# A four-layer graph network on one core: aggregations as seven products with the adjacency as left factor, three graphs in flight in tiles handed out by the plan

## The chip, the core and the metric

The kernel runs on one core of a Trainium2 chip. The engines are TensorE (PE; its weight loads are shown as PEld), VectorE (DVE), ScalarE (ACT), GpSimd (POOL) and SyncE (SP, which issues the large DMAs). The metric is the device time of one execution in microseconds (us). Everything is float32.

## The reference

32 graphs of 512 nodes with 256 features each go through four layers; each layer multiplies by the graph's own 512 x 512 adjacency matrix. `_layernorm` has no gain or shift.

```
x = _layernorm(x + mlp0((1 + eps) * x + adj @ x))           # relu(h @ W1 + b1) @ W2 + b2, 256-512-256
x = _layernorm(x + prelu(adj @ (x @ W.T + b)))              # 256-256
h = layer_norm(x, gamma, beta)
x = _layernorm(x + (x + relu((adj @ h) @ W_rel + b_rel + h @ W_root)))
x = _layernorm(x + silu(rmsnorm((epsilon * x + adj @ x) @ W1 + b1) * w) @ W2 + b2)   # 256-1024-256
```

## The kernel before

The kernel writes no instruction directly. It describes operations (`plan.do`, `plan.move`), and `Plan.add` derives what depends on what from the tiles that an operation reads and writes. This is done by grains: 128 columns of a tile, PSUM tiles included. Matmuls into one bank are in addition kept in order (`ordered=o.bank`). `Plan.order` then lays all operations out in time with a duration for each kind (`matmul_time`, `vector_time` and so on), always giving an engine the operation of the oldest graph that is ready; an operation that two engines can do goes to the one that would finish first. The operations are issued in the order found, so each engine's queue has a fixed order, and the semaphores follow from that order. In the profile all operations therefore bear one line, L180, and are told apart by their tiles.

Two graphs are in flight. Each has its own `Set` of named tiles (adjT, x, aT, h, t, part0 and others); graph b uses set b % 2. `load_graph` issues x and four chunks of the adjacency on SP. PSUM has eight tiles `ps`, one bank of 128 x 512 each, and the plan gives an operation the bank that comes free first.

A layer begins with an aggregation. `aggregate` is called twice, for each half of the features. It sums four matmuls, 128 x 128 of x as stationary operand and 128 x 512 of the transposed adjacency as moving operand, into one bank, and a copy takes the bank to the tile aT (features on partitions, 512 nodes). Layers 0 and 3 need the adjacency with something added on its diagonal: GpSimd copies the four 128 x 128 diagonal blocks to dg, adds, restores and adds again. Layer 1 also sums the adjacency's rows on GpSimd. After the aggregation come dense matmuls with the layer's weights, element work on VectorE and ScalarE, and a norm (`Norm`: statistics, a power on GpSimd, and four `tensor_scalar` on VectorE in `scaled`).

Layer 3 already does its two dense products by the seven-product scheme of Strassen and Winograd. `seven` calls `product` for m1 to m7, `take` where a partial sum has to be kept in SBUF, and `put` where a block of the result is made; weights are combined once (`weight_sums`), the right factor for each graph. Its three accumulators x, y and z are three banks; m1, m6, m7 and m4 are added up in x one after the other. In the first product of layer 3 an accumulator is a whole bank (two blocks of 256 columns), in the second half of a bank is used.

Of the kernel before, what the change touches and what calls it, by code (L numbers as in the profile page):

```python
# [16 lines left out]
GRAIN = 128  # L17
BANKS = 8


def span(ap):

    n = 1
    for d in ap.shape[1:]:
        n *= d
    return n

# [42 lines left out]
@dataclass  # L70
class Op:


    rank: tuple
    ways: dict
    banks: list
    behind: int = 0
    ready: dict = field(default_factory=dict)
    then: list = field(default_factory=list)
    start: float = 0.0  # L80
    way: str = ""


class Bank:


    def __init__(self):
        self.index = None
        self.left = 0
        self.until = 0.0  # L90


class Part:


    def __init__(self, bank, model, path):
        self.bank, self.model, self.path = bank, model, path
        self.shape = model.shape

    def __getitem__(self, i):  # L100
        return Part(self.bank, self.model[i], (*self.path, i))

    def place(self, tiles):
        shape, *path = self.path
        v = tiles[self.bank.index]
        if shape:
            v = v.rearrange("p (i n) -> p i n", i=shape)
        for i in path:
            v = v[i]
        return v  # L110


class Plan:
# [3 lines left out]
    def __init__(self, nc, banks):  # L117
        self.nc = nc
        self.tiles = banks
        self.ops = []  # L120
        self.place = 0
        self.writer, self.readers = {}, {}

    def bank(self, split=0):
        model = self.tiles[0]
        if split:
            model = model.rearrange("p (i n) -> p i n", i=split)
        return Part(Bank(), model, (split,))

    def grains(self, x):  # L130
        key = x.bank if isinstance(x, Part) else x.tensor.name
        ap = x.model if isinstance(x, Part) else x
        starts = [ap.offset]
        dims = list(ap.ap)[1:]
        for step, n in dims[:-1]:
            starts = [s + step * i for s in starts for i in range(n)] if step else starts
        step, n = dims[-1]
        return {
            (key, g)
            for s in starts  # L140
            for g in range(s // GRAIN, (s + step * (n - 1)) // GRAIN + 1)
        }

    def add(self, ways, out, ins, ordered=None):
        op = Op((self.place, len(self.ops)), ways, [])
        self.ops.append(op)
        before, behind_end = set(), set()
# [4 lines left out]
        for g in reads:  # L152
            if g in self.writer:
                behind_end.add(self.writer[g])
        for g in reads - writes:
            self.readers.setdefault(g, []).append(len(self.ops) - 1)
        for g in writes:
# [3 lines left out]
            self.writer[g] = len(self.ops) - 1  # L161
        me = len(self.ops) - 1
        before = (before | behind_end) - {me}
        for i in before:
            self.ops[i].then.append((me, i in behind_end))
        op.behind = len(before)
        for x in (out, *ins):
            if isinstance(x, Part) and x.bank not in op.banks:
                op.banks.append(x.bank)
                x.bank.left += 1  # L170

    def do(self, ways, out, *args, ordered=None, **kw):

        ins = [x for x in (*args, *kw.values()) if isinstance(x, (bass.AP, Part))]

        def issue(engine, method, more):
            def put(x):
                return x.place(self.tiles) if isinstance(x, Part) else x

            getattr(getattr(self.nc, engine), method)(  # L180
                put(out), *(put(x) for x in args), **{k: put(x) for k, x in kw.items()}, **more
# [4 lines left out]
                e: (times, lambda e=e, method=method, more=more: issue(e, method, more))  # L186
                for e, (method, times, more) in ways.items()
# [4 lines left out]
    def move(self, engine, out, src, times, tile_in=None):  # L192

        self.add(
            {engine: (times, lambda: getattr(self.nc, engine).dma_start(out, src))},
            None if tile_in is not None else out,
            [] if tile_in is None else [tile_in],
        )

    def order(self):  # L200
        free = dict.fromkeys(("tensor", "vector", "scalar", "gpsimd", "sync"), 0.0)
        occupant = [None] * BANKS
        open_ops = {i for i, op in enumerate(self.ops) if not op.behind}
        done = []
        while open_ops:
            best = {}
            spare = min(
                (0.0 if o is None else o.until if not o.left else 1e12, k)
                for k, o in enumerate(occupant)
            )  # L210
            for i in open_ops:
                op = self.ops[i]
                wait = spare[0] if any(b.index is None for b in op.banks) else 0.0
                at = {e: max(free[e], wait, op.ready.get(e, 0.0)) for e in op.ways}
                way = min(at, key=lambda e: at[e] + sum(op.ways[e][0]))
                best.setdefault(way, []).append((at[way], op.rank, i))
            t, engine = min((min(c)[0], e) for e, c in best.items())
            assert t < 1e11, "no bank comes free"
# [5 lines left out]
            for b in op.banks:  # L224
                if b.index is None:
                    b.index = spare[1]
                    occupant[b.index] = b
                b.left -= 1
                b.until = max(b.until, t + busy + then)
            for n, reads in op.then:  # L230
                o = self.ops[n]
                o.behind -= 1
                for e in o.ways:
                    if e != engine:
                        at = t + busy + then + HAND[e]
                    elif e == "tensor" or not reads:
                        at = 0.0
                    else:
                        at = t + busy + then + HAND[e]
# [10 lines left out]
def tile_gnn_stack(ctx: ExitStack, tc: tile.TileContext, a: dict, out: bass.AP):  # L250
# [36 lines left out]
    STREAMS = 2  # L287
# [4 lines left out]
    plan = Plan(nc, [psum.tile([P, N], F32, tag=f"ps{i}", name=f"ps{i}") for i in range(BANKS)])  # L292


    def on_vector(method, n, **more):
        return {"vector": (method, vector_time(n), more)}

    def either(method, n, **more):
        return {
            "vector": (method, vector_time(n), more), "gpsimd": (method, gpsimd_time(n), more)  # L300
        }

    def mm(o, lhsT, rhs, first, last):
        n = rhs.shape[-1]
        ways = {"tensor": ("matmul", matmul_time(n), dict(start=first, stop=last, skip_group_check=True))}
        plan.do(ways, o, lhsT, rhs, ordered=o.bank)

    def flip(o, x):
        ways = {"tensor": ("transpose", flip_time(P), {})}
        plan.do(ways, o, x, ident, ordered=o.bank)  # L310

    def act(o, x, func, **kw):
        plan.do({"scalar": ("activation", scalar_time(span(o)), dict(func=func))}, o, x, **kw)

    def copy(o, x):
        plan.do(
            {
                "scalar": ("activation", scalar_time(span(o)), dict(func=AF.Copy)),
                "vector": ("tensor_copy", vector_time(span(o)), {}),
            },  # L320
            o, x,
        )

    def add(o, x, y, ways=on_vector):
        plan.do(ways("tensor_add", span(o)), o, x, y)

    def sub(o, x, y, ways=on_vector):
        plan.do(ways("tensor_sub", span(o)), o, x, y)

    def mul(o, x, y):  # L330
        plan.do(on_vector("tensor_mul", span(o)), o, x, y)

    def ts(o, x, s1, s2, op0, op1=None):
        more = dict(op0=op0) if op1 is None else dict(op0=op0, op1=op1)
        plan.do(on_vector("tensor_scalar", span(o), **more), o, x, s1, s2)

    def stt(o, x, s, y, op0, op1):
        plan.do(on_vector("scalar_tensor_tensor", span(o), op0=op0, op1=op1), o, x, s, y)

    def on_gpsimd(method, n, **more):  # L340
        return {"gpsimd": (method, gpsimd_time(n), more)}

    def inv_sqrt(o, x):
        n = span(o)
        plan.do(
            {"gpsimd": ("tensor_tensor", power_time(n), dict(op=ALU.pow))}, o, x, mhalf[:, 0:n]
        )

# [18 lines left out]
    def weight(name):  # L367
        w = a[name]
        t = constant(name, [P, w.shape[0] // P, w.shape[1]])
        plan.move("sync", t, w.rearrange("(c p) f -> p c f", p=P), move_time(w.shape[0] * w.shape[1] / 256))  # L370
# [11 lines left out]
    class Set:  # L382
# [3 lines left out]
        def __init__(self, number):  # L386
            self.number = number
            self.slots = {}

        def __call__(self, slot, shape):  # L390
            size = 1
            for n in shape:
                size *= n
            if slot not in self.slots:
                self.slots[slot] = work.tile(
                    [P, SLOTS[slot]], F32, tag=f"{slot}_{self.number}", name=f"{slot}{self.number}"
                )
            t = self.slots[slot][:, 0:size]
            if len(shape) == 2:
                t = t.rearrange("p (i n) -> p i n", i=shape[0])  # L400
            return t

        def tok(self, slot):
            return self(slot, [NC, D])

        def feat(self, slot, n=DC):
            return self(slot, [n, N])

    SLOTS = dict(
        adjT=NC * N, x=NC * D, dg=N, xb=NC * D, aT=DC * N, r=NC * D, h=FC3 * N, x2=NC * D,  # L410
# [406 lines left out]
```

## Time and profile before

| What | us |
|---|---|
| median of 3 runs (2618.21 to 2622.77) | 2622.53 |
| the profiled execution | 2623.28 |
| its span, first to last instruction | 2621.4 |
| aggregation matmuls, "ps<-adjT,x", 2048 records, busy | 941.6 |
| mean length of one such record | 0.598 |
| all of DVE, busy | 1779.3 |
| all of POOL, busy | 790.8 |
| all of ACT, busy | 696.4 |

An f32 matmul leaves two records, each with a weight load of its own. Records of matmuls overlap: each lasts from its start until its last column has left the array, while the next one begins earlier. What a matmul costs is therefore read from one start to the next. The granted TensorE clock is 0.994 of full speed on average.

### The profile page before, as it was taken

The numbers are of one execution on the slowest core, as the hardware profiler recorded it, in microseconds if no ns is written. First come the engines' busy times: TensorE is split into PE (matmuls) and PEld (weight loads), VectorE is DVE, ScalarE is ACT, GpSimd is POOL, SyncE is SP. The second block draws the span as 40 slices with busy tenths as digits, with TensorE's granted clock in tenths as the row PEclk, the third lists the DMA queues.
The fourth block names the chain that finished last, engine by engine and source line by source line (L and its number), as shares of the span: only waits on it lengthen the run. The fifth ranks groups of instructions, "written<-read, shape, count | busy, mean of one in ns | idle before, by whom it ended". The sixth has DMA issues, their size and how long they took to land.

```text
span 2621.4 us, 30535 instructions
## 1 busy us (share of the span) xinstructions
PE 2578.0 (98%) x11400; PEld 1807.3 (69%) x11400; DVE 1779.3 (68%) x3956; ACT 696.4 (27%) x1186; POOL 790.8 (30%) x1063
## 2 busy tenths in 40 slices
PE   7999999999999999999999999999999999999996
PEld 4766667666777677676767776666766677767765
DVE  4666667766676666766667666666776667666675
ACT  1231232322223222232213322123232222322222
POOL 3233232333332233322332313323233333223311
PEclk9999999999999999999999999999999999999998
DMA  3000000000001000000100100100010000010000
GB/s 117 25 33 33 9 32 25 33 33 33 9 25 33 33 33 9 33 33 25 33 12 29 33 25 33 33 9 33 25 33 33 33 9 25 33 33 33 9 9 9
DMA packets 34884, 73.54 MB, mean 28 GB/s; under 512 B 6832, under 2 KB 9648, under 8 KB 34736
## 3 DMA queue, kind: packets, MB, share of 16 engines
q1 hardware_dynamic: 30576, 71.05, 8.1%
q8 instruction: 90, 1.47, 0.2%
q10 hardware_dynamic: 4160, 0.54, 0.1%
q14 instruction: 58, 0.48, 0.1%
HBM read 54.80 MB, written 16.78 MB: 27 GB/s over the span
## 4 chain that ended last, share of the span: by engine, by line
PE 91%; DVE 6%; ACT 1%; POOL 1%; issue 1%; DMA 0%; POOLq 0%; ACTq 0%; DVEq 0%
PE ps L180 91%; DVE t L180 2%; POOL rstd L180 1%; ACT part L180 1%; DVE r L180 1%; DVE st L180 1%; DVE mv L180 0%; DVE h L180 0%; DVE x L180 0%; DMA L_gnn_b_c<-in_L_gnn_b_dram 0%; DVE ve L180 0%; ACT h L180 0%; DMA adjT<-in_adj_dram 0%; DVE part L180 0%; ACT u L180 0%
## 5 line engine op out<-in xcount | busy, mean ns | idle before, releaser
L180 PE MATMUL ps<-adjT,x 128*128 128x512 f32 x2048 | 941.6, 598 | 21.5 <-POOL adjT L180 13.6
L180 PEld LDWEIGHTS ps<-adjT,x 128*128 128x128 f32 x2048 | 376.2, 192 | 389.0 <-issue 323.9
L180 POOL TENSOR_TENSOR rstd<-ve,mhalf 128x4 f32<-128x4 f32 (+1 forms) x160 | 191.5, 1197 | 918.4 <-DVE ve L180 916.3
L180 PEld LDWEIGHTS ps<-L_gnn_W,h 128*128 128x128 f32 x2560 | 391.2, 192 | 107.3 <-issue 57.8
L180 PE MATMUL ps<-L_gnn_W,h 128*128 128x128 f32 (+1 forms) x2560 | 441.5, 318 | 4.1 <-ACT h L180 2.8
L180 PE MATMUL ps<-aT,L_gnn_W 128*128 128x512 f32 (+1 forms) x1024 | 361.1, 486 | 0.0
L180 DVE COPY aT<-ps 128x512 f32<-128x512 f32 x194 | 133.8, 690 | 256.7 <-PE ps L180 256.7
L180 ACT ACTIVATE part<-ps,L_gnn_b_c 128x256 f32<-128x256 f32 x384 | 157.2, 471 | 547.8 <-PE ps L180 547.8
L180 DVE TENSOR_SCALAR x<-r,mv,rstd 128x256 f32<-128x256 f32 x512 | 249.0, 541 | 72.1 <-POOL rstd L180 72.1
L180 PEld LDWEIGHTS ps<-aT,L_gnn_W 128*128 128x128 f32 x1024 | 193.5, 190 | 135.8 <-issue 123.4
L180 POOL TENSOR_TENSOR xb<-x,L_gnn_b 128x256 f32<-128x256 f32 x256 | 186.5, 751 | 205.8 <-DVE part L180 106.0
L180 DVE TENSOR_TENSOR h<-ps,part 128x512 f32<-128x512 f32 x192 | 132.8, 691 | 134.3 <-PE ps L180 74.4
L180 ACT ACTIVATE h<-ps,L_gnn_b_c 128x256 f32<-128x256 f32 (+1 forms) x256 | 141.8, 579 | 289.1 <-PE ps L180 259.8
L180 ACT ACTIVATE h<-h,L_gnn_rms_weight_c 128x512 f32<-128x512 f32 x256 | 168.8, 714 | 155.6 <-DVE h L180 154.8
L180 DVE BATCH_NORM_STATS2 st<-r 128x6 f32<-128x256 f32 x512 | 206.9, 409 | 3.9
L180 DVE TENSOR_TENSOR h<-h,ps 128x512 f32<-128x512 f32 x256 | 161.3, 683 | 2.3 <-PE ps L180 2.3
L180 POOL TENSOR_TENSOR adjT<-dg,loop 128x128 f32<-128x128 f32 x256 | 120.8, 472 | 139.6 <-PE ps L180 129.9
L180 POOL COPY adjT<-dg 128x128 f32<-128x128 f32 x128 | 76.9, 603 | 213.7 <-PE ps L180 213.7
L180 PE MATMUL ps<-t,L_gnn_W 128*128 128x256 f32 x512 | 140.0, 386 | 0.8 <-DVE h L180 0.8
L180 DVE TENSOR_TENSOR t<-ps,u 128x512 f32<-128x512 f32 x64 | 44.3, 692 | 141.1 <-PE ps L180 141.1
L180 PE MATMUL ps<-t,A 128*128 128x256 f32 x512 | 134.7, 386 | 2.1
L180 PE MATMUL ps<-L_gnn_W_root,h 128*128 128x256 f32 x512 | 121.1, 379 | 0.2 <-ACT h L180 0.2
(79 smaller groups left out, 3011.5 us busy)
## 6 DMA issues: line engine op xcount, KB each, us to landing
adjT<-in_adj_dram SPq DMA_DIRECT2D x128, 256.0 KB, 3.2
x<-in_x_dram SPq DMA_DIRECT2D x32, 512.0 KB, 4.9
out_dram<-x SPq DMA_DIRECT2D x32, 512.0 KB, 2.6
L_gnn_W<-in_L_gnn_W_dram SPq DMA_DIRECT2D x2, 1024.0 KB, 9.0
L_gnn_W<-in_L_gnn_W_dram SPq DMA_DIRECT2D x2, 512.0 KB, 6.5
L_gnn_b<-in_L_gnn_b_dram ACTq DMA_DIRECT2D x3, 128.0 KB, 6.0
L_gnn_W<-in_L_gnn_W_dram SPq DMA_DIRECT2D x1, 256.0 KB, 4.4
L_gnn_W_rel<-in_L_gnn_W_rel_dram SPq DMA_DIRECT2D x1, 256.0 KB, 3.3
```

What stands on the lines that cost most here:

```text
L180: getattr(getattr(self.nc, engine), method)(put(out), *(put(x) for x in args), **{k: put(x) for k, x in kw.items()}, **more)
```

## The change

Aggregation becomes one call that makes both halves of the features by seven products instead of eight. The adjacency's blocks are the left factor, whose sums are made once per graph; the right factor's sums are made for each layer from x. Each product is two matmuls of 256 columns into half a bank; x and y are the halves of one bank, z and w of another. There is now a fourth accumulator w for m4, which is put with a saved part of x. The order of the products is new.

```diff
+    def seven(x, y, z, w, product, take, put):
         product("m1", x, True)
         t1 = take(x, 0, 0, 0)
-        product("m2", y, True)
-        put(y, t1, 0, 0)
         product("m5", z, True)
         t5 = take(z, 1, 1, 1)
+        product("m4", w, w.room is not z.room)
+        t4 = take(w, 1, 0, 2)
         product("m6", x, False)
-        t6 = take(x, 0, 1, 0)
+        t6 = take(x, 0, 1, 3)
+        product("m2", y, y.room is not x.room)
+        put(y, t1, 0, 0)
         product("m3", z, False)
         put(z, t6, 0, 1)
         product("m7", x, False)
         put(x, t5, 1, 1)
-        product("m4", x, False)
-        put(x, None, 1, 0)
+        put(x, t4, 1, 0)
+    def left_sums(left, a21, s):
+        sub(s[2], left["m1"], a21, vector, gpsimd)
+        add(s[0], a21, left["m4"], vector, gpsimd)
+        sub(s[1], s[0], left["m1"], vector, gpsimd)
+        sub(s[3], left["m2"], s[1], vector, gpsimd)
+        left.update(m5=s[0], m6=s[1], m7=s[2], m3=s[3])
+    def right_sums(b11, b12, b21, b22, t):
+        sub(t[0], b12, b11)
+        sub(t[1], b22, t[0])
+        sub(t[2], b22, b12, vector, gpsimd)
+        sub(t[3], b21, t[1], vector, gpsimd)
+        return dict(m1=b11, m2=b21, m3=b22, m4=t[3], m5=t[0], m6=t[1], m7=t[2])
+    def aggregate(x, adjacency):
+        aT = room(DC, N)
...
+        def product(m, ps, first):
+            for k in range(HC):
+                mm(ps, right[m][:, k, :], adjacency.left[m][:, k, :], first and k == 0, k == HC - 1)
+        def take(ps, i, k, n):
+            copy(parts[:, n, :], ps)
+            return parts[:, n, :]
+        def put(ps, t, i, k):
+            add(aT[:, k, i * TH : (i + 1) * TH], ps, t)
+        xy, zw = bank(2, TH), bank(2, TH)
+        seven(xy[:, 0, :], xy[:, 1, :], zw[:, 0, :], zw[:, 1, :], product, take, put)
```

`Adjacency` loads the four chunks, makes the four left sums (`sums`), and keeps, changes and restores the diagonals of m1's and m4's blocks and of two of the sums. Row sums for layer 1 use one of the left sums. Layer 3's first product has four whole banks (`bank(2, TH)`) for x, y, z, w; its second, `xy, zw = bank(4, P), bank(4, P)`, shares two like the aggregation.

The named sets are gone. `Room` stands for a tile that the plan picks when the first operation that uses it is laid out: 34 rooms of 1024 columns, 12 small ones, eight banks. Three graphs may be in flight, and a younger graph must leave some rooms free:

```diff
+    banks = pool(psum, "ps", 8, N, P, (0, 2, 2))
+    rooms = pool(work, "room", ROOMS, NC * D, P, (0, 6, 10))
+    smalls = pool(work, "few", SMALL, 64, 4, (0, 2, 4))
...
+        PERIOD, PACE = 80.0, 2.0
+        work, need = {}, []
+        for op in self.ops:
+            t = op.ways.get("tensor")
+            need.append(work.get(op.graph, 0.0) * PACE if t else 1e3)
+            if t:
+                work[op.graph] = work.get(op.graph, 0.0) + t[0][0]
...
+                    need[i] = min(need[i], need[n] - cost)
+            op.rank = (op.graph * PERIOD + need[i], i)
```

An engine now takes the ready operation with the earliest due time by `rank` instead of the oldest graph's. Some operations may newly go to a second engine: the scaling of a norm to ScalarE (`AF.Identity` with a shift that VectorE computes), the adjacency's sums, diagonals and row sums to GpSimd, VectorE or ScalarE as the operation allows.

## The prediction

> **What bounds the kernel now.** I read the page first (busy shares, then the chain), then the groups with shapes kept apart, then a timeline of six microseconds in layer 3, then the busy time in windows.
>
> ```profile
> span 2621.4 us, 30535 instructions
> PE 2578.0 (98%) x11400; PEld 1807.3 (69%) x11400; DVE 1779.3 (68%) x3956; ACT 696.4 (27%) x1186; POOL 790.8 (30%) x1063
> PE 91%; DVE 6%; ACT 1%; POOL 1%; issue 1%; DMA 0%; POOLq 0%; ACTq 0%; DVEq 0%
> ```
>
> PE is never idle: 98% busy and 91% of the chain that ended last. "Busy" can hide waits, so I go to starts.
>
> ```profile
> 1055.66 0.59 PE L180 MATMUL ps<-adjT,x 128*128 128x512 f32 x1
> 1056.09 1.03 PE L180 MATMUL ps<-aT,L_gnn_W 128*128 128x256 f32 x4
> 1056.95 0.59 PE L180 MATMUL ps<-t,L_gnn_W 128*128 128x256 f32 x2
> 1057.15 1.21 ACT L180 ACTIVATE part<-ps,L_gnn_b_c 128x256 f32<-128x256 f32 x3 [21.85 <-PE ps L180]
> ...
> 1059.81 1.03 PE L180 MATMUL ps<-aT,A 128*128 128x256 f32 x4
> 1060.01 0.84 ACT L180 ACTIVATE part<-ps,L_gnn_b_c 128x256 f32<-128x256 f32 x2 [0.39 <-PE ps L180]
> 1060.90 0.73 PEld L180 LDWEIGHTS ps<-t,A 128*128 128x128 f32 x4 [0.47 <-ACT part L180]
> 1060.90 1.13 PE L180 MATMUL ps<-t,A 128*128 128x256 f32 x4
> ```
>
> Two things stand here. First the price of a matmul: one f32 matmul leaves two records; a 512-column record takes 0.43 us start to start (1055.66 to 1056.09), and four 256-column ones 0.86 us (1056.09 to 1056.95), 0.216 each. Column for column, 256 costs what 512 does. At these rates all matmul records of the span together are worth 2541.6 us (2560 at 0.429, 4360 at 0.216, 4479 at 0.112, which is what the narrowest cost). The first starts at 13.6 us. Of the other 66 us about 40 lie at the end, where the last graph runs alone (32 between matmuls, 8.5 after the last one), and 5 in the first two periods of 82 us; that leaves some 0.7 us of loss in each of the other periods.
>
> Second, **how a half-used bank behaves**. The product at 1056.09 is two matmuls, one for each half of one PSUM bank. ACT had been idle for 21.85 us and wants the first half, complete after two records (about 1056.70). It starts at 1057.15, 0.04 us after the fourth record's end (1056.73+0.38). And at 1060.90 PE begins to rewrite the first half of a bank whose first ACT read ended at 1060.48; it has nothing else to do from 1060.67, but starts 0.05 us after the read of the *second* half (1060.01+0.84=1060.85). So a read of one half waits for writes to the other half, and a write for reads of it.
>
> ```profile
> core 0: us, PE busy (x) PEld busy (x) DVE busy (x) ACT busy (x) POOL busy (x), PEclk, DMA share, GB/s
> 1000.00:1082.00 82.00, 81.87 (x349) 56.74 (x348) 53.03 (x122) 19.24 (x35) 24.78 (x31) 1.00 0.08 26
> 2482.00:2560.00 78.00, 71.47 (x332) 52.22 (x330) 55.90 (x132) 17.86 (x31) 12.45 (x14) 0.98 0.02 7
> 2560.00:2622.00 62.00, 42.02 (x196) 32.27 (x196) 31.20 (x64) 16.00 (x28) 7.29 (x8) 0.79 0.02 9
> ```
>
> One graph takes 82 us; only the last one, alone, lets PE stand, and there the granted clock falls to 0.79.
>
> **The matmuls removed.** An aggregation is now 8 matmuls of 512 columns: 16 records x 0.429 = 6.86 us. After, seven products of two 256-column matmuls: 28 records x 0.216 = 6.05 us. The gain is 0.816 us in each of 128 aggregations (4 layers, 32 graphs): **-104.5 us**. All of it is on PE's path. Weight loads rise from 16 to 28 an aggregation; 256-column records already run at 0.216 us behind a load each (190 ns, "ps<-t,A"), so that costs nothing; without this cover, nearly their own length.
>
> **Work added elsewhere**, by rows of the groups:
>
> ```profile
> L180 DVE COPY aT<-ps 128x512 f32<-128x512 f32 x194 | 133.8, 690 | 256.7 <-PE ps L180 256.7
> L180 DVE TENSOR_TENSOR r<-ps,part 128x256 f32<-128x256 f32 x96 | 40.7, 424 | 43.8 <-PE ps L180 43.6
> L180 DVE TENSOR_TENSOR t<-aT 128x256 f32<-128x256 f32 x64 | 29.2, 456 | 1.1
> L180 DVE TENSOR_TENSOR t<-aT,t 128x256 f32<-128x256 f32 x64 | 35.0, 547 | 1.1
> ```
>
> For a graph on DVE: 16 puts x 0.424 = 6.8; first two operand sums, 8 x 0.50 = 4.0; one more put for each of two steps in layer 3's first product, 2 x 0.69 = 1.4, and one more take in its second, 0.4; five shifts of the norms at 0.16 = 0.8; away go the copies to aT, 133.8/32 = 4.2. Fixed: +9.2 us. Movable to ACT or POOL, if on DVE: 16 takes x 0.42, 8 more operand sums x 0.456, 4 adjacency sums x 0.69 (the 512-column adds), loops and row sums about 2: 15.2. Movable away: 20 norm scalings, up to 10.8. From 1779.3/32 = 55.6 DVE comes to between 54 and 80, near 67 us a graph. POOL's diagonal work (238.5 us in three groups) doubles in elements, +7.5 us a graph, on 24.7; ACT takes about 10 more on 21.8. None exceeds PE's 2437/32 = 76 us except DVE's upper end. I take 0 for throughput. SP's loads keep count and size (x and four adjacency chunks a graph, 3 to 5 us to landing); with a period of 75 us or more to land in, also behind an output or while waiting for a free room, they cost 0.
>
> **The wait added.** Aggregation and the second product of layer 3 now hold x and y in one bank, z and w in the other. The plan orders matmuls within a bank, but lets readers go by 128-column grains: for it, taking z and writing w are unrelated. By the rows above they are not. The order m1 m5 m4 m6 m2 m3 m7 puts m4 (w) right behind m5 (z), and m2 (y) right behind m6 (x). The take of z, planned 0.29 us after m5, falls inside m4; PE must stop within m4 until it is over. Price, from 1059.81 to 1060.90: 1.09 us with two ACT reads of 0.84, so 0.25 for drain and two handovers, plus one read of 0.42: **0.67 us**. Lower end 0, when another graph's matmuls lie between. Behind a waiting m4 stand all later matmuls of all three graphs (PE runs in order), and behind those the DVE and ACT operations that read them. Pairs a graph: 2 in each of 4 aggregations, 2 in layer 3, 10; in all 320: 0 to 214 us. I take 0.4 for the four m5/m4 pairs of the aggregations (m4's operand is third in a chain of DVE sums, so PE has often gone to another graph for one matmul of 0.43), and 0.6 for the other six (m2 waits for nothing in the plan; layer 3's operands are long made): 5.2 us a graph, **+166 us**.
>
> m7 writes x while the put of y may still read: m3's 0.86 us lies between, more than the 0.67, so only a late DVE shows. 0 to 0.67, five times a graph; at 0.1: **+16 us**. Third graph in flight: it could win at most the 0.7 us a graph that steady state loses, 22 us, or lose as much through the stricter reserve of rooms; I take 0. Start: the adjacency sums and diagonals of graph 0 come before its first product, 0 to 5 us, I take 3. End: the last graph alone, with sums ahead and two puts (0.85) for a copy (0.69), 0 to 12, I take 6.
>
> A rule of the Trainium skill speaks against this change. The rows show PE against ACT in one bank; the page "PSUM — Partial Sum Buffer" (section "PSUM bank collisions raise a hardware error") says that any two of PE, ACT and DVE must be kept apart within a bank, whatever the columns, and by semaphores. By it every one of the 320 pairs hands over in full unless covered, which at 0.67 would make 2757 us; by the plan's grains the pairs would be free and the sum 2543. No run yet shows ACT against DVE.
>
> **Sum**: 2621.4 - 104.5 + 166 + 16 + 3 + 6 = 2707.9. The profiled execution took 2623.3, 1.9 more than its span, and the median is 2622.5: +1.1 gives **2709 us**.
>
> **Rivals.**
> *The pairs are covered* (not slower). With three graphs ready, PE would go to another graph between m5 and m4, m6 and m2. For it: a period of two graphs leaves hardly any PE idle now. Against: the plan picks by due time, and an aggregation comes just after a norm, when its graph is behind and is served alone. It decides from a mean stall of (104.5-25)/320 = 0.25 us down. With 0.05 a pair and m7 covered: 2621.4-104.5+16+9+1 = 2543.
> *DVE becomes the bound.* At its upper end 80 us a graph, 2560, plus the 13.6 and 40 us at the ends: 2614 by itself, about no change. But DVE then also waits its turn in the banks: with half of the pairs' 166 us, and 3 us of DVE idle a graph (about 96), some 2614+83+96 = 2793. Against: the plan may give 15 us to ACT and POOL, which are 27% and 30% busy.
> *The change doesn't do what it says*, 256-column products costing more than half of 512: excluded by 0.216 against 0.429.
>
> **Chances and range.** Forecast 0.62, covered pairs 0.27, DVE 0.11. The forecast's own range is 2630 (mean stall 0.25 to 0.3) to 2770 (all at 0.67). The whole range reaches into the covered case and stops short of the worst of DVE: 2540 to 2795. No change would be within 0.2% (5 us), about what the runs tell apart: 0.04, taken from between the cases. Faster 0.27, slower 0.69.
>
> **What would show it.** Right: some 3584 more 256-column records at 0.216 and 2048 fewer of 512; PE waits of 0.3 to 0.7 us released by ACT or DVE, about 10 a graph, with the reader of the other half ending 0.05 us before PE goes on; a PE that idles 5 to 6 us a graph. Wrong: PE back to back through m5, m4, m6, m2 with takes running beside it; idle PE with DVE over 90% busy (the third case); or granted clock below 0.99 through the middle, which I have not priced.

## The result and the profile after

The changed kernel takes 2899.79 us (median of 4 runs, 2899.09 to 2904.38) against 2622.65 for the kernel before: 1.1065 times as long, 95% interval 1.1046 to 1.1084. The forecast was 2709, its range 2540 to 2795. The direction was right, and the loss is three times as large: 277 us instead of 86.

The page of the kernel after: span, engines, and the chain that ended last by engine.

```profile
span 2902.6 us, 35439 instructions
PE 2634.1 (91%) x12936; PEld 2112.5 (73%) x12936; DVE 2153.9 (74%) x4994; ACT 1047.6 (36%) x1978; POOL 845.6 (29%) x801
PE 49%; DVE 43%; issue 4%; ACT 3%; DMA 1%; SPq 0%; POOL 0%; POOLq 0%; ACTq 0%; DVEq 0%
```

The chain has turned over. It lay on PE for 91%; now DVE holds 43% of it, though DVE is busy for only 74% of the span. An engine that isn't full but stands in the chain is one that others wait for at the wrong moments.

The waits of the kernel after: who waited for whom, us in total, how often, the longest.

```profile
DVE room L216 <- PE ps L216: 465.0, 586, 6.9
...
PEld ps L216 <- DVE room L216: 338.0, 371, 12.9
PE ps L216 <- DVE room L216: 215.1, 323, 12.9
...
PEld ps L216 <- ACT room L216: 86.3, 136, 4.4
```

Before, no line of PE waiting for DVE was above 34 us; this was the largest:

```profile
PEld ps L180 <- DVE x L180: 33.8, 82, 4.9
```

Now PE's weight loads and matmuls wait for DVE in 694 entries (a load and its matmul can stand for the same stop), and DVE waits for PE 586 times.

Where the time went can be counted in PE's records, each at its price start to start (0.429, 0.216 and 0.112 us, the medians in both traces). At these prices the matmuls are worth 2541.6 us before and 2437.2 after, so the 104.5 us are there. What starts later than these prices allow is a gap. Of the gaps, waits make 364 us after (46 before), matmuls that ran while the trace has the granted clock at half 44 (7), and 47 (9) are a restart that I had not priced: after a wait, the second record starts 0.32 us after the first, not 0.216. Together that is 392 us more, against 281.2 + 104.5 = 385.7 by the spans.

Taking PE's records in order against the matmuls in the kernel's plan tells which product waits. In the aggregations m4 stands for 141 us, m2 for 75 and m1 for 50; m4 in layer 3's own products for 53. So m4 and m2, the two products that follow one in the other half of their bank, hold over half. Not all of m4's wait is the bank's: at least 57 of its 141 us end with an operand sum on DVE, not with a take.

Taking the records of DVE, ACT and POOL in the plan's order too tells which operation ended last before each stop of PE. Of 360 us in stops above 0.1 us, 145 end with a reader of the other half of a shared bank, 18 with ACT reading the other half in layer 3's first product (whose accumulators are whole banks of two blocks, before as after), 158 with an operand that was not yet made (137 of them made on DVE), and 17 with a reader that the plan knew. So there are two causes of about the same size. Four microseconds of the trace (timeline, kernel after; start, length, what, idle before and releaser):

```profile
1043.74 1.99 PE L216 MATMUL ps<-room,room 128*128 128x256 f32 x8 [0.47 <-ACT room L216]
1044.48 0.39 ACT L216 ACTIVATE room<-ps 128x256 f32<-128x256 f32 x1 [0.79 <-PE ps L216]
...
1045.77 0.42 DVE L216 COPY room<-ps 128x256 f32<-128x256 f32 x1 [0.71 <-PE ps L216]
1046.11 0.16 DVE L216 TENSOR_SCALAR few<-few 128x4 f32<-128x4 f32 x1
1046.25 1.16 PEld L216 LDWEIGHTS ps<-room,room 128*128 128x128 f32 x6 [0.92 <-DVE room L216]
1046.25 2.05 PE L216 MATMUL ps<-room,room 128*128 128x256 f32 x8 [0.52 <-DVE room L216]
```

The first row merges eight records: two of the end of m4, four of m6 and the first two of m2, which make one matmul. The copy at 1045.77 takes m6's half. m6's last record is over at 1045.30, and DVE is free. But m2's first matmul is writing the other half; the copy starts 0.04 us after that one has left the array, and m2's second matmul waits until 0.05 us after the copy's end. PE was free from 1045.57: 0.68 us, and the restart adds 0.10. The trace has both stops as waits for a semaphore: the copy waits for the one that m2's first matmul raises, and m2's second matmul for the one that the copy raises. So the program that was issued keeps PE and DVE apart in a bank, while the plan that ordered it did not reckon with that; what the chip would do without these semaphores no run shows.

DVE's part shows in the groups with shapes kept apart (count, busy us, mean ns, idle before):

```profile
L216 DVE TENSOR_TENSOR room<-room,room 128x512 f32<-128x512 f32 x353 | 299.5, 848 | 9.7 <-DMA room<-in_adj_dram 5.5 <-ACT room L216 3.7
...
L216 DVE TENSOR_TENSOR room<-ps,room 128x512 f32<-128x512 f32 x384 | 255.4, 686 | 210.5 <-PE ps L216 125.4 <-ACT room L216 83.2
```

The same sum of 512 columns takes 0.686 us when one operand comes from PSUM and 0.848 when both come from SBUF. Of the 353, the 184 that ran beside POOL (busy for over 30% of their length) took 1.005 us on average and the other 169 0.678. Over all of DVE's operations the excess over the undisturbed length is 261 us, 119 before. Over half of that before lay in the norm scalings (kernel before):

```profile
L180 DVE TENSOR_SCALAR x<-r,mv,rstd 128x256 f32<-128x256 f32 x512 | 249.0, 541 | 72.1 <-POOL rstd L180 72.1
```

The 280 of them that ran clear of POOL took 0.409 us on average, the 232 beside it 0.700.

### The profile page after: what moved, and what is told of

Read it like the earlier page. It is cut to its first block, busy times and chain, and to the rows that moved or that the text cites. A ratio compares the mean times of both kernels' runs of the same rounds, so it can differ in the third digit from the quotient of the medians.

```text
span 2902.6 us, 35439 instructions
## 1 busy us (share of the span) xinstructions
PE 2634.1 (91%) x12936; PEld 2112.5 (73%) x12936; DVE 2153.9 (74%) x4994; ACT 1047.6 (36%) x1978; POOL 845.6 (29%) x801
## 4 chain that ended last, share of the span: by engine, by line
PE 49%; DVE 43%; issue 4%; ACT 3%; DMA 1%; SPq 0%; POOL 0%; POOLq 0%; ACTq 0%; DVEq 0%
PE ps L216 49%; DVE room L216 38%; DVE few L216 5%; ACT room L216 3%; DMA room<-in_adj_dram 1%; SPq L232 0%; DMA L_gnn_eps<-in_L_gnn_eps_dram 0%; POOL few L216 0%; DVE A L216 0%; DVE L_gnn_W L216 0%; POOL room L216 0%; ACT L216 0%; POOLq L954 0%; DVE L_gnn_W_rel L216 0%; DVE L_gnn_W_root L216 0%
## 5 line engine op out<-in xcount | busy, mean ns | idle before, releaser
L216 PE MATMUL ps<-room,room 128*128 128x256 f32 x3584 | 965.0, 408 | 183.2 <-DVE room L216 156.6
L216 PEld LDWEIGHTS ps<-room,room 128*128 128x128 f32 x3584 | 659.6, 198 | 412.6 <-DVE room L216 254.9
L216 DVE TENSOR_TENSOR room<-ps,room 128x256 f32<-128x256 f32 (+1 forms) x1152 | 553.0, 504 | 347.5 <-PE ps L216 260.9
L216 PE MATMUL ps<-L_gnn_W,room 128*128 128x128 f32 (+1 forms) x3584 | 632.7, 323 | 34.7 <-DVE room L216 26.2
L216 PEld LDWEIGHTS ps<-L_gnn_W,room 128*128 128x128 f32 x3584 | 545.6, 193 | 107.0 <-DVE room L216 38.5
L216 POOL TENSOR_TENSOR room<-room,room 128x512 f32<-128x512 f32 (+1 forms) x219 | 265.2, 1211 | 1092.2 <-ACT room L216 743.4
L216 PE MATMUL ps<-room,L_gnn_W 128*128 128x256 f32 (+1 forms) x1536 | 505.6, 453 | 4.2
L216 ACT ACTIVATE room<-ps,L_gnn_b_c 128x256 f32<-128x256 f32 (+1 forms) x640 | 306.4, 514 | 533.4 <-PE ps L216 531.8
L216 DVE TENSOR_TENSOR room<-room,room 128x512 f32<-128x512 f32 (+1 forms) x645 | 467.2, 725 | 11.6 <-DMA room<-in_adj_dram 5.5
L216 PEld LDWEIGHTS ps<-room,L_gnn_W 128*128 128x128 f32 x1536 | 285.4, 190 | 122.9 <-issue 78.7
```

The lines of the kernel that those rows point to most:

```text
L216: getattr(getattr(self.nc, engine), method)(put(out), *(put(x) for x in args), **{k: put(x) for k, x in kw.items()})
```

## The experiments

All kernels compute the whole reference. Times are medians against the kernel before of the same session (2618.5 to 2620.4). Every edit makes the plan lay out all operations anew, so a small part of a difference can come from the new order alone.

**A plan that knows the bank** (e1_plan_knows):

```diff
-    banks = pool(psum, "ps", 8, N, P, (0, 2, 2))
+    banks = pool(psum, "ps", 8, N, N, (0, 2, 2))
```

> The same work as after; only the plan changes: a PSUM bank is one grain of 512 columns, so the plan knows that a matmul into one half of a bank waits for a reader of the other half, and can put other graphs' matmuls there. Theory A (halves of a bank shared, unknown to the plan: PE's stalls after, 441 us in gaps over 0.1 us, start at m4 behind m5 and at m2 behind m6, and the rest is DVE coming late behind them): stalls fall to 60 to 180 us, time 2540 to 2680. Theory B (DVE, 74% busy against 68%, is itself too slow for the plan, and PE waits for its sums): a better-informed plan doesn't make DVE faster; time 2780 or more.

2694.25 us, ratio 1.0289 (1.0270 to 1.0308). 205 us are won by telling the plan one fact; the program computes the same, in another order and with some operations on another engine. The time is 14 us above theory A's bracket and far below theory B's; 235 us of gaps are left, more than A's 180.

**Products in an order that alternates between the banks** (e2_order), m1 m5 m2 m4 m6 m3 m7:

```diff
         product("m5", z, True)
         t5 = take(z, 1, 1, 1)
+        product("m2", y, y.room is not x.room)
+        put(y, t1, 0, 0)
         product("m4", w, w.room is not z.room)
         t4 = take(w, 1, 0, 2)
         product("m6", x, False)
         t6 = take(x, 0, 1, 3)
-        product("m2", y, y.room is not x.room)
-        put(y, t1, 0, 0)
```

> After with the products in the order m1 m5 m2 m4 m6 m3 m7, so that no product follows one in the other half of its own bank; banks, plan and work as in after. Theory A: the handovers m5 to m4 and m6 to m2 lie under a product of 0.86 us in the other bank; at 0.67 us each 200 to 320 us of the stalls go, time 2580 to 2700. m4 also comes one product later, so its operand, the last of three DVE sums, has 0.86 us more: theory B allows some 60 us from that alone, time 2820 to 2850.

2855.59 us, 1.0896 (1.0875 to 1.0918): 44 us won, theory A's expectation missed. The aggregations' waits at m2 went (6 us in place of 75), but layer 3's m6 alone now waits 114 us, mostly for the take of m1 and the put of y, both readers of m6's own bank. With two products a bank, every product has a reader of its bank behind it; alternating moves the handover on, and any delay on DVE exposes it. The granted clock was lower too, 0.962 against 0.976, so part of what the order won was lost again.

**A bank for each accumulator** (e3_four_banks); the order is that of after:

```diff
-        xy, zw = bank(2, TH), bank(2, TH)
-        seven(xy[:, 0, :], xy[:, 1, :], zw[:, 0, :], zw[:, 1, :], product, take, put)
+        seven(*(bank(TH) for _ in range(4)), product, take, put)
...
-        xy, zw = bank(4, P), bank(4, P)
...
+        seven(*(bank(HC, P) for _ in range(4)), product, take, put)
```

> After with a bank for each of x, y, z and w in the aggregations and in the second product of layer 3; the order of products is that of after, and no bank is shared by halves. It needs four banks at once instead of two. Theory A: no handover is left that the plan doesn't know; time 2530 to 2620, the forecast's 2621 less 104.5 us plus what the ends and a denser DVE cost. Theory B: DVE's work is unchanged, so 2780 or more. If four banks at once are too many for three graphs, PE waits for free banks: 2620 to 2750.

2662.31 us, 1.0157 (1.0140 to 1.0174): 237 us won. In the aggregations m2 falls from 75 to 2 us and m4 from 141 to 18. But the time lies above theory A's bracket. It is within that for missing banks, yet no stop in the trace ends with a bank coming free. The waits that are left are for readers and results on DVE and ACT: layer 3's m3 and m6 for takes (27 and 24 us), m1 for a norm's scaled x (26 us where ACT made it, 20 where DVE did). So a second cause is there. It is smaller here than in after: stops that end with an operand not yet made fall from 158 to 94 us, though DVE has nearly the same work. Part of DVE's lateness came with the shared banks.

**Both** (e4_both: alternating order, a bank as one grain):

> The order of products that alternates between the two banks, and a plan that takes a bank as one grain. Theory A: as good as or better than either alone, 2540 to 2640. Theory B: 2780 or more.

2732.11 us, 1.0426 (1.0411 to 1.0442), 38 us slower than the grain alone and between the two expectations. The alternating order isn't a cure even when the plan knows.

**Four banks, POOL relieved of two-operand sums** (f1_sums_on_dve): the operand sums, adjacency sums, diagonals, row sums and sums of squares lose `gpsimd` as an engine, for instance

```diff
-        sub(t[2], b22, b12, vector, gpsimd)
-        sub(t[3], b21, t[1], vector, gpsimd)
+        sub(t[2], b22, b12)
+        sub(t[3], b21, t[1])
```

> Four banks as in e3_four_banks, and no two-operand sum may go to POOL any more except the one that adds a row to x (operand sums, adjacency sums, diagonals, row sums, squares: all on DVE). DVE gets some 150 us more of work by the plan. Theory C (a DVE operation with both operands in SBUF is slowed while POOL runs: in after 128x512 sums take 0.68 us alone and 1.00 us beside POOL, operations that read PSUM are not slowed; the plan knows nothing of it and DVE comes late): the mean 128x512 sum falls from 0.825 to below 0.74 us, PE's stalls fall from 204 us by 30 to 100, time 2560 to 2640. If DVE's amount of work is what counts: 2680 or more.

2634.67 us, 1.0056 (1.0039 to 1.0073): 28 us faster with more work on DVE. The mean 512-column sum falls from 0.825 to 0.716 us (e3_four_banks, then f1_sums_on_dve):

```profile
L216 DVE TENSOR_TENSOR room<-room,room 128x512 f32<-128x512 f32 x354 | 291.9, 825 | 15.2 <-DMA room<-in_adj_dram 8.6 <-ACT room L216 5.7
L216 DVE TENSOR_TENSOR room<-room,room 128x512 f32<-128x512 f32 x480 | 343.5, 716 | 8.2 <-ACT room L216 4.0 <-DMA room<-in_adj_dram 3.9
```

The gaps fall from 204 to 177 us, 27 where theory C expected 30 to 100; the time is within its range, at the weak end. It speaks against the theory that DVE's amount of work counts.

**Four banks, longer times in the plan** (f8_slow_dve):

```diff
-    return 0.06 + n * 0.00106, 0.085
+    return 0.10 + n * 0.00116, 0.085
...
-                    scalar(AF.Identity, D, r, scale=scale, bias=shift[:, c : c + 1]),
+                    scalar(AF.Identity, D + 128, r, scale=scale, bias=shift[:, c : c + 1]),
```

> Four banks, and the plan is given longer times: DVE 0.10 + n x 0.00116 us instead of 0.06 + n x 0.00106, and 0.1 us more for a norm's scaling on ACT, which takes 0.49 us start to start against 0.39 in the plan. The instructions are the same kinds; only engines chosen and order change. If what is left in e3_four_banks is DVE and ACT coming later than the plan thinks: time 2560 to 2630, PE's stalls 100 to 170 us. If DVE is at its limit the plan's times don't matter: 2650 or more.

2674.47 us, 1.0206 (1.0190 to 1.0222): 12 us slower than without, the expectation missed. The time lies where DVE at its limit would have put it; k1_all below, with DVE busier and PE hardly waiting, speaks against that reading. Why longer times in the plan cost time here wasn't found out.

**Four banks, two graphs in flight** (f4_flight2: `FLIGHT = 2`):

> Four banks, but only two graphs in flight. If the third graph is what covers the longer chains (sums, takes, puts) of the seven products: slower than e3_four_banks by 100 us or more, 2760 to 2950. If two graphs are enough, as before the change: 2640 to 2690.

3217.86 us, 1.228 (1.2246 to 1.2315). The third graph is worth 556 us here; without it PE is busy for 85% of the span instead of 94%. It is not idleness alone: PE spent 586 us at half clock, against 47 with three graphs.

**Four banks, grain and milder times** (h5_mid: grain as in e1, DVE 0.08 + n x 0.0011 and 0.1, ACT's scaling as in f8):

> Four banks, a bank as one grain of the plan (which still matters for layer 3's first product, where ACT reads one half while PE writes the other), a norm's scaling on ACT 0.1 us longer, and DVE at 0.08 + n x 0.0011 us with 0.1 us of latency. If all of what is left are times and waits that the plan doesn't know: 2530 to 2610, faster than before. If DVE is at its limit: 2640 or more.

2622.50 us, 1.0008 (0.9999 to 1.0018): level with before, between the two expectations. PE's gaps are 162 us; 31 of them are m4 in layer 3's aggregation waiting for its operand sum.

**Four banks in the aggregations only** (e3a_agg_only: the first part of e3's diff):

> After with four banks in the aggregations only; the second product of layer 3 keeps its two shared banks. The 237 us that four banks in both places won divide by the stalls after had at the products concerned: m4 and m2 of the aggregations 216 us, m4, m6, m7 and m3 of layer 3 about 113 (some of them in its first product). If the handovers are the cause: 2690 to 2780, nearer the lower end if the plan fills them. If the rearranged plan as such is what helped: within 20 us of e3_four_banks, 2640 to 2680.

2806.96 us, 1.0718 (1.0700 to 1.0735): 93 us won, above the bracket. The shared banks that remain, 32 second products of layer 3, cost the other 145 us, 4.5 us a graph, against 1.2 in my sum. m4 in layer 3's products waits 99 us here, and 18 in e3. Stops that end with a reader of the other half of a shared bank come to 118 us, so the larger part of the 145 can be seen directly.

**All of it** (k1_all): four banks, the grain, sums on DVE, the times of h5, and the order m1 m2 m5 m6 m4 m3 m7:

> All causes found so far taken away: four banks, a bank as one grain of the plan, no two-operand sum on POOL but the row adds, longer times for DVE and for the scaling on ACT in the plan, and the products in the order m1 m2 m5 m6 m4 m3 m7, which gives the operand sums of m5, m6 and m4 0.9 to 1.7 us more. If handovers and DVE's lateness are all that ate the 104.5 us: 2540 to 2600, faster than before. If DVE, then 82% busy, is at its limit: 2610 or more.

2520.39 us, 0.9624 (0.9609 to 0.9638): 98 us faster than before and the fastest kernel of the study. Its page and windows:

```profile
span 2520.4 us, 35823 instructions
PE 2462.0 (98%) x12936; PEld 2104.4 (83%) x12936; DVE 2130.9 (85%) x5334; ACT 1024.8 (41%) x1953; POOL 453.7 (18%) x486
PE 83%; DVE 7%; DMA 6%; issue 3%; SPq 1%; ACT 0%; POOL 0%; POOLq 0%; DVEq 0%; ACTq 0%
```

```profile
core 0: us, PE busy (x) PEld busy (x) DVE busy (x) ACT busy (x) POOL busy (x), PEclk, DMA share, GB/s
...
1000.00:1082.00 82.00, 81.82 (x427) 69.49 (x427) 70.71 (x179) 33.09 (x63) 14.07 (x15) 1.00 0.14 45
```

```profile
L216 DVE TENSOR_TENSOR room<-room,room 128x512 f32<-128x512 f32 x480 | 328.5, 685 | 44.8 <-ACT room L216 25.2 <-DMA room<-in_adj_dram 19.2
...
L216 DVE TENSOR_TENSOR room<-ps,room 128x512 f32<-128x512 f32 x384 | 252.5, 684 | 143.2 <-PE ps L216 81.9 <-ACT room L216 55.8
```

DVE is busier than in any other kernel here, 85%, and holds PE up least: PE is idle for 0.2 us in 82. The sums of two SBUF operands take 0.685 us, as long as those from PSUM. PE's gaps are 64 us, 58 before.

**h5_mid in that order** (k2_order: k1_all with the sums on either engine):

> h5_mid with the order m1 m2 m5 m6 m4 m3 m7. In h5_mid PE still stands about 46 us at layer 3's m4 and m5, the first waiting for the operand sums on DVE. If that wait is one of order: 2560 to 2605. If DVE is late by its amount of work, the wait moves to another product: 2610 to 2640.

2594.85 us, 0.9906 (0.9889 to 0.9922): the order is worth 28 us, and keeping POOL's sums costs 74 against k1_all, which differs in nothing else. That edit does two things: it lets DVE's sums run undisturbed, and it spares POOL's own longer time for a sum. Only 7 us of PE's stops here end with a result of POOL, so its own lateness is a small part.

**After with only DVE's part cured** (l1_dve_cured: f1's edit and the times of h5, on after's shared banks):

> After with only DVE's part changed: all two-operand sums but the row adds on DVE, longer times for DVE and for the scaling on ACT in the plan. Banks shared by halves, the plan's grains and the order of products stay as in after. e3_four_banks is the opposite: handovers gone, DVE as it was. If the two causes add up (237 us for the banks; for DVE 2662 to 2520 less what order and grain bring, some 70 to 140): 2760 to 2830. If DVE's lateness is what makes the handovers long: 2650 to 2720.

2747.39 us, 1.0486 (1.0470 to 1.0501): 152 us won, 13 us below the bracket for two causes that add up. The edit joins the sums on DVE and the plan's longer times; what each gave wasn't tried on these banks.

**k1_all with the shared banks put back** (l3_shared):

> k1_all with the two shared banks put back (and the plan's grain in PSUM at 128 columns), all else equal. Each aggregation has two hidden handovers again, m1 to m2 in the middle of a bank and m4 to m3, and the second product of layer 3 too: 320 pairs. At my 0.67 us uncovered and half of them covered, 105 to 215 us: 2625 to 2735. If handovers are harmless once DVE is in time: 2520 to 2570.

2777.73 us, 1.0596 (1.0569 to 1.0624): two shared banks that the plan doesn't know cost 257 us, above the bracket, or 0.80 us for each of the 320 pairs if it is spread over them. (The plan's finer grain came back with them; in e1 a plan that knows the banks won 205 us.) Stops that end with a reader of the other half of a shared bank make 226 us of it, where k1_all has none. The costliest group of PE here waits for DVE and ACT:

```profile
L216 PE MATMUL ps<-room,room 128*128 128x256 f32 x3584 | 921.0, 398 | 172.5 <-DVE room L216 97.4 <-ACT room L216 75.2
```

In k1_all the same group has 32.7 us of idle time before it.

The four corners: after 2900; banks cured 2662 (-237); DVE cured 2747 (-152); both, with the order and the grain, 2520 (-379, where 237 + 152 = 389). Each cause is shown by taking it away. That they simply add up is not: the last corner has the order and the grain besides, and the order alone was worth 28 us where it was tried. The traces show that they feed each other: curing the banks (e3) also took 64 us off the waits for operands, and curing DVE (l1) took 23 off the waits for the other half of a bank.

## Why the prediction was right and wrong

- *The matmuls removed, -104.5 us*: right, 2541.6 to 2437.2 in PE's records; k1_all has nearly all of it (its span is 101 us shorter than that of before).
- *The wait added, the mechanism*: right, and now shown for DVE too. A plan that tracks halves of a bank, and semaphores that give a bank one user at a time, make the stop foretold, with the foretold 0.04 and 0.05 us of handover.
- *The wait added, +166 us*: counted at the stops of after, this term and m7's below were about right, 145 us and 22 of restart against 182 together. By what their removal gains they were too small: 237 (e3 against after) to 257 (l3 against k1). With the stops gone, the waits for operands and the time at half clock (142 us in after, 47 in e3) fell too. The upper end of 0.67 us a pair was no upper end: a stop costs 0.68 plus 0.10 of restart, and a late reader makes it longer. The reason given for the m5/m4 pairs, that PE has often gone to another graph, was wrong: in 119 of the 128 aggregations m4's matmuls follow m5's at once. That the bank's part of m4's 141 us is 63, 0.49 a pair, near my 0.4, is partly luck: where the operand sum was late, which I had counted as cover, it was a wait of its own. For m2 I said 0.6 and the trace has 0.585, restart included.
- *"I take 0 for throughput"*: this is the step that failed. DVE came to 67.3 us a graph, my 67, and below PE's 76; but engine totals don't bound a fixed order. An operation that ends late by half a microsecond stops PE if PE's next matmul needs it. In the trace of after 158 us of PE's stops end with an operand that was not yet made, where the sum has 0 (all of PE's waits together were 46 us before); cured, DVE's part gave 152 us. The sign was in the rows I used, "t<-aT,t" at 547 ns beside "r<-ps,part" at 424, and the norm scalings ("x<-r,mv,rstd") at 541 ns, which took 409 clear of POOL and 700 beside it.
- *m7 behind a late put, +16 us*: about right; layer 3's m7 behind that put stands for 20 us.
- *Third graph, 0*: as a difference to before it can't be told apart, but it is no small term: 556 us on four banks, half clock included.
- *The rivals*: the covered pairs were wrong. "DVE becomes the bound" had a true core, lateness, and a wrong reason, its amount of work: k1_all runs at 85% DVE with 64 us of gaps, against 58 before.
- *Granted clock*, named as not priced: 0.976 on average; PE spent 142 us at half clock, 31 before, which lengthened matmuls by 37 us more. Before, half clock came with PE standing (the last graph), and e3 and k1_all have 47 and 32 us of it, so it goes with the waits.

## What to carry to other kernels

Track PSUM by whole banks in any hand-made order or planner: putting two accumulators into one bank saves a bank and costs PE a full evacuation, here 0.8 us, each time its next matmul writes one while the other is read. In a fixed order, price operations as they run beside the other engines, and look at what ends just before PE starts again, not at engine totals. When a plan and the measured time disagree by much, ask first which wait the plan doesn't know.

## What the runs showed of the hardware

Moving work *to* the busier engine made the kernel faster. A DVE sum with both operands in SBUF takes 0.68 us alone and 1.00 us beside POOL; one that reads PSUM takes 0.69 in both cases (0.685 and 0.689 in the kernel after). The Trainium skill says on the page "SBUF — State Buffer", section "Who interferes with whom", that DVE's second SBUF input goes through a port that it shares with GpSimd. The durations agree. What this and POOL's own time for the sums cost a PE-bound kernel together is the step from k2_order to k1_all, 74 us.

A stop of PE costs more than its length: at full clock the first 256-column record after it lasts 0.483 us instead of 0.379, and the second starts 0.104 us late, in the kernel before as in the kernel after.
